# Filler matmuls in TensorE's idle stretches, bias rows by an eight-column matmul, more buffers for raw weights, and a new order

## The chip, the core and the metric

The kernel runs on one core of one Trainium2 chip. The metric is device time in microseconds (us). The kernel before was run three times: 3003.74, 3004.77 and 3006.28 us, so its median is 3004.77 us. The execution that the hardware profiler recorded took 3005.68 us; its instructions span 3004.0 us of that.

## What is computed

A stack of four graph layers works on 32 independent graphs ("batches") of 512 nodes with 128 features. Each graph has a 0/1 adjacency matrix `adj` of 512 x 512 with about 16 neighbours a node.

```python
h = relu(layernorm(x)); x = x + L0(h)   # max over neighbours j of relu(h@(W1-W2) at i + h@W2 at j + b)
h = relu(layernorm(x)); x = x + L1(h)   # 4 layers; each: src/dst aggregates by normalised adj, then
                                        #   tanh(concat(src_agg, self, dst_agg) @ wu + bu)
h = relu(layernorm(x)); x = x + L2(h)   # (adj / row sum) @ (h @ weight) + bias
h = relu(layernorm(x)); x = x + L3(h)   # 4 GRU steps: m = adj.T @ (h @ w3[l]); gates of m and h
# in L1: src = nodes @ ws + bs;  dst = nodes @ wd + bd;  self = nodes @ wn + bn
```

The weights are shared by all batches. In L1 the products `ws@wu`, `wn@wu` and `wd@wu` are formed once, and so are the bias rows `bs@wu` and `bd@wu`.

## The kernel before

`batch(b)` describes the whole work of one graph: `prepare` (load `x` and `adj`, first layer norm, a transposed adjacency `at`, counts `cc` copied across partitions into `ccd`, and the eight keys a row that name neighbours), `gathers` (28 gathers of rows `G` from a table in device memory by GpSimd, and 32 one-hot products `pa` by TensorE, both folded by maxima on VectorE into `gm` and `acc`), `layer1` (four layers with aggregates `pg` over `at` and `an`, and products `pu`), and `layer23` (layer 2, then four GRU steps with `pk`, `pg`, `phn` and `pxn`).

Nothing runs in the order in which it is written. `Flow` notes every operation with a cost and its dependencies. `step` then plays a small model of the five engines and issues, from those that could start first, the one with the earliest due time; `LEADS` shifts the due times of stages, `LAST` those of the last batches, and `PACE` sets the distance from batch to batch. Line 496 issues all of them, so nearly every row of the profile has line 496, and a row is told by its tiles. Each engine takes its instructions strictly in the order that comes out of this.

The weights enter the same flow as two more parts, `first` and `rest` (lines 1187 to 1188), with places `WEIGHTS` ahead of batch 0. In `rest`:

- the bias vectors are loaded into `brow` row by row, all on SyncE's DMA queue (line 663), transposed by one matmul `pb` and copied to `bcol`;
- for each of the four layers `wu`, then `ws`, `wn`, `wd` are loaded (lines 681 and 685), all three into the one buffer with the tag "f", transposed (`pwt`), copied (`wt`, tag "gate0"), multiplied (`pw`) and copied to `w1`;
- for each layer `pv` holds `bs@wu` and `bd@wu` as single rows of one partition. They are split into a rounded part and a remainder (`both`, lines 708 to 712), and eight small DMAs on SyncE's queue (lines 713 to 719) spread the four rows, twice each, over eight partitions of `b8`;
- then come the layer 2 weights, `w3`, and the eight GRU matrices `graw`, which share one buffer with the tag "gate1" (line 739).

The product `pu` of layer 1 reads `b8` with eight rows of scaling values `rows`. GRU step `l` of a batch is one long chain: transposes `ph`, rounding to `hi` and `lo`, eight passes `pg`, the copy `mT`, two `pk` and one `pxn` product, then `nn` and `h` on VectorE and ScalarE, and the next `ph`. The two first halves of `pk` and `phn` read only `h`.

PSUM has eight banks, shared by four users (`BANKS`, `Share`).

## Time and profile before

| item | value |
|---|---|
| median of 3 runs | 3004.77 us (3003.74 to 3006.28) |
| profiled execution | 3005.68 us, span 3004.0 us, mean granted TensorE clock 0.979 |
| TensorE matmul | 2821.0 us busy, 94% of the span |
| VectorE | 2403.8 us, 80% |
| GpSimd | 1798.9 us, 60% |
| ScalarE | 1214.9 us, 40% |
| chain that ended last | TensorE 77%, VectorE 12%, issue 4%, ScalarE 2%, DMA 1%, GpSimd 1% |

Times in the trace count from the start of the span. A busy time is the sum of an engine's instructions, and the granted clock is the share of full speed that the throttle gave TensorE. In the page's strip of 40 slices a slice is 75 us, and a digit is a tenth.

The batches can be followed by the group that writes `xo`, the last arithmetic of a batch: it ends its batches at 307.2 us (batch 0), 759.0 (batch 5), 2583.4 (batch 26), 2914.5 (batch 30) and 2993.1 (batch 31), each time the start of its fourth instruction. From batch 5 to batch 26 that is 1824.4 / 21 = 86.9 us a batch.

### The profile page before, as it was taken

The page shows a single profiled execution, that of the slowest core. Times are in us where ns is not written, and L with a number is a line of the kernel's source. Part 1 is how long each engine was busy: PE and PEld are TensorE (multiplying, and loading weights), DVE is VectorE, ACT ScalarE, POOL GpSimd, SP SyncE. Part 2 cuts the span into 40 slices and gives each one's busy share as a digit, 9 for nine tenths or more (in the row PEclk, how much of TensorE's full clock was granted, in tenths as well). Part 3 has the DMA queues.
Part 4 walks back from the last instruction along what each step waited for, and adds up shares of the span by engine and source line. Part 5 has one row for each costly group of instructions (what it writes and reads, how often), then busy time and mean ns, then how long its engine had stood idle before and what let it go on. Part 6 is the DMA issues. An engine that isn't in the chain of part 4 may idle for free.

```text
span 3004.0 us, 37228 instructions
## 1 busy us (share of the span) xinstructions
PE 2821.0 (94%) x11233; PEld 1741.0 (58%) x11233; DVE 2403.8 (80%) x5364; ACT 1214.9 (40%) x2516; POOL 1798.9 (60%) x2000
## 2 busy tenths in 40 slices
PE   4688989999999999999999999999999999999985
PEld 3455656666666666666666666666666666655542
DVE  5887879888888988888888888888988888886422
ACT  2333434444444434444444434444434444432322
POOL 3666666666666666666666666666666666655211
PEclk7899999999999999999999999999999999999997
DMA  5533343433344334333433433344333334333000
GB/s 142 122 80 67 77 84 74 82 69 67 71 85 85 81 73 84 60 64 86 85 83 73 85 61 71 76 84 85 75 80 79 66 64 85 67 57 58 11 4 5
DMA packets 192289, 218.42 MB, mean 73 GB/s; under 512 B 31401, under 2 KB 140625, under 8 KB 192081
## 3 DMA queue, kind: packets, MB, share of 16 engines
q0 software_dynamic: 47104, 92.34, 22.2%
q1 hardware_dynamic: 77392, 64.90, 7.2%
q10 hardware_dynamic: 67584, 58.73, 6.3%
q8 instruction: 91, 1.49, 0.2%
q14 instruction: 118, 0.96, 0.1%
HBM read 164.32 MB, written 17.96 MB: 61 GB/s over the span
## 4 chain that ended last, share of the span: by engine, by line
PE 77%; DVE 12%; issue 4%; ACT 2%; DMA 1%; POOL 1%; ACTq 0%; SPq 0%; DVEq 0%; POOLq 0%
PE pg L496 23%; PE pu L496 18%; PE pk L496 15%; PE pa L496 6%; PE phn L496 4%; PE pxn L496 4%; DVE acc L496 3%; PE pkey L496 2%; PE pf L496 2%; PE ph L496 1%; DVE qhl L496 1%; DVE nn L496 1%; DVE x L496 1%; PE pc L496 1%; PE pt L496 1%
## 5 line engine op out<-in xcount | busy, mean ns | idle before, releaser
L496 POOL DMA_INDIRECT G<-qtab,idx x768 | 824.6, 1074 | 602.6 <-DVE gm L496 487.9
L496 DVE TENSOR_TENSOR acc<-acc,pa 128x512 f32<-128x512 f32 x992 | 674.2, 680 | 146.7 <-PE pa L496 134.0
L496 PE MATMUL pa<-oh,qhl 128*128 128x512 f32 x1024 | 472.6, 515 | 12.5 <-DVE oh L496 6.7
L496 PE MATMUL pg<-an,hi 128*128 128x512 f32 x1024 | 461.3, 451 | 1.1 <-ACT hi L496 0.7
L496 PE MATMUL pu<-ag,w 128*128 128x512 f32 x896 | 449.9, 596 | 1.1 <-DVE ag L496 1.1
L496 PE MATMUL pg<-an,lo 128*128 128x512 f32 x1024 | 435.2, 426 | 0.7 <-POOL lo L496 0.7
L496 DVE TENSOR_SCALAR oh<-ccd 128x1024 fp32r<-128x1024 bf16 x512 | 401.2, 802 | 10.3 <-PE pa L496 10.3
L496 PE MATMUL pg<-at,hi 128*128 128x512 f32 x640 | 289.1, 452 | 13.9 <-ACT hi L496 9.2
L496 PE MATMUL pg<-at,lo 128*128 128x512 f32 x640 | 297.0, 465 | 3.4 <-POOL lo L496 2.8
L496 PEld LDWEIGHTS pa<-oh,qhl 128*128 128x128 f32 x1024 | 197.2, 194 | 147.0 <-issue 52.5
L496 PE MATMUL pk<-h,g_hh 128*128 128x512 f32 x512 | 262.7, 618 | 4.4 <-DVE acc L496 1.9
L496 DVE TENSOR_TENSOR gm<-gm,G 128x128 f32<-128x128 f32 x768 | 260.8, 340 | 3.9 <-DMA G<-qtab,idx 3.1
L496 ACT ACTIVATE xn<-x,shift,rstd 128x128 f32<-128x128 f32 x512 | 212.4, 484 | 110.1 <-POOL shift L496 109.4
L496 PEld LDWEIGHTS pg<-an,hi 128*128 128x128 f32 x1024 | 194.0, 189 | 95.5 <-issue 50.7
L496 PEld LDWEIGHTS pg<-an,lo 128*128 128x128 f32 x1024 | 193.9, 189 | 87.0 <-issue 40.9
L496 PE MATMUL pk<-mT,g_ih 128*128 128x512 f32 x512 | 240.8, 593 | 2.2 <-ACT mT L496 2.2
L496 ACT COPY mT<-pg 128x512 f32<-128x512 f32 x160 | 93.7, 585 | 354.6 <-PE pg L496 354.0
L496 PEld LDWEIGHTS pu<-ag,w 128*128 128x128 f32 x896 | 166.9, 190 | 114.5 <-issue 82.2
L496 ACT ACTIVATE gate<-pk,bsum 128x512 f32<-128x512 f32 x256 | 175.4, 686 | 139.2 <-PE pk L496 132.2
L496 POOL TENSOR_TENSOR rstd<-rstd,mhalf 128x4 f32<-128x4 f32 x128 | 145.9, 1140 | 139.4 <-DVE shift L496 138.6
L496 ACT CAST hi<-ph 128x512 fp32r<-128x512 f32 x96 | 56.2, 586 | 382.2 <-PE ph L496 382.2
L496 DVE TENSOR_TENSOR ag<-pg,rbc 128x512 f32<-128x512 f32 x256 | 174.5, 682 | 21.3 <-PE pg L496 18.2
(161 smaller groups left out, 5043.3 us busy)
## 6 DMA issues: line engine op xcount, KB each, us to landing
af<-in_adj_dram ACTq DMA_DIRECT2D x32, 1024.0 KB
ccd<-cc SPq DMA_DIRECT2D x512, 64.0 KB
an<-in_adj_dram POOLq DMA_DIRECT2D x128, 256.0 KB, 4.3
x<-in_x_dram ACTq DMA_DIRECT2D x64, 256.0 KB
rbc<-scal SPq DMA_DIRECT2D x32, 512.0 KB
G<-qtab,idx POOLq DMA_INDIRECT x768, 3.8
qtab<-qn SPq DMA_DIRECT2D x128, 64.0 KB
out_dram<-xo ACTq DMA_DIRECT2D x32, 256.0 KB
```

The costliest lines, as they stand in the source:

```text
L496: op.fn(*(real(v) for v in op.args), **{k: real(v) for k, v in op.kw.items()})
```

## The change

Five things change. `clock` is called before each TensorE instruction is placed: it issues `n` filler matmuls ("spin": constants times constants, 128x512, bf16, into an unused PSUM bank) when the model has TensorE idle for over 1 us, and it follows the throttle in the model, whose matmul costs now depend on it. The bias rows are made by matmuls with eight columns, `bm`, so that each row comes out on the partitions where it is wanted; the 32 small DMAs and the `both` tiles are gone. The raw weights get more buffers, and half of the weight loads go to ScalarE's DMA queue. `rest` is cut in two, with the later half, `last`, placed at -3.0. `PACE`, `LEADS` and `LAST` have new values, and so has the modelled cost of a DMA.

```diff
-PACE = 45.29
+PACE = 45.28
 LEADS = {
...
-    "gather0": 21.0, "gather1": 4.8, "gather2": 6.6, "gather3": -2.6,
-    "first": 14.3, "layer1": -15.8, "layer10": -31.7, "layer11": -34.7,
+    "gather0": 21.0, "gather1": 4.8, "gather2": 6.6, "gather3": -2.7,
+    "first": 14.9, "layer1": -15.8, "layer10": -31.7, "layer11": -34.7,
     "layer12": -17.6, "layer13": -49.5, "layer2": 17.3, "layer3": 7.8,
-    "layer30": 58.6, "layer31": 78.0, "layer32": 33.2, "layer33": 37.4,
-    "out": 22.6,
+    "layer30": 58.6, "layer31": 78.0, "layer32": 36.2, "layer33": 30.6,
+    "out": 18.1,
 }
-LAST = (0.0, 0.0, 0.06, -0.57, -0.08)
-WEIGHTS = (-4.52, -3.22)
+LAST = (0.0, 0.0, -0.31, -0.67, 0.62)
+WEIGHTS = (-4.52, -3.22, -3.0)
...
+    SPIN, IDLE = 0.23, 1.0
+    WINDOW = 3.413
...
-                return 0.4, 2.0 + outs[0].size() * width / 1.5e5
+                return 0.48 if engine == "sync" else 0.42, 2.0 + outs[0].size() * width / 1.2e5
...
+        if op.engine == "pe":
+            t = self.clock(op, t)
         cost = op.cost + (self.EVENT * max(0, len(need) - 1) if op.engine != "pe" else 0.0)
+        if op.engine == "pe":
+            cost /= self.rate
+            self.active += cost
...
+    def clock(self, op, t):
+        gap = t - self.free["pe"]
+        n = int(0.7 * (gap - 0.4) / self.SPIN)
+        if self.spin and gap > self.IDLE and n > 0:
+            ring = next(r for r in self.rings.values() if r.tag == "idle")
+            spare = [b for b in ring.slots if b is None or (not b.left and b.end < t)]
+            if spare:
+                view, work = self.spin(n)
+                buf = view.tile
+                buf.real = ring.give(buf)
+                for args in work:
+                    self.nc.tensor.matmul(*(real(v) for v in args), start=True, stop=True)
+                buf.end = t
+                self.active += n * self.SPIN
+        while t >= (self.window + 1) * self.WINDOW:
+            share = self.active / self.WINDOW
+            if share < 0.42:
+                self.rate = 0.5
+            elif share > 0.84:
+                self.rate = 1.0
+            self.window += 1
+            self.active = max(0.0, self.active - self.WINDOW)
+        return t
...
-            F.sync.dma_start(out=brow[at : at + m, :], in_=src)
+            (F.sync, F.act)[len(col) % 2].dma_start(out=brow[at : at + m, :], in_=src)
...
-        b8 = self.temp("hg", "b8")
+        self.b8 = self.own([8, NL1, P], F32R, "b8r")
+        bm = self.own([P, NL1, 2, 8], F32, "bm")
+        F.pool.memset(bm, 0.0)
+        for i in range(NL1):
+            for k, nm in enumerate(("bs", "bd")):
+                c = col[nm, i]
+                F.act.copy(bm[:, i, k, k::2], bcol[:, c : c + 1].to_broadcast([P, 4]))
...
-                w = self.temp("f", f"{nm}{i}")[:, 0:ch, :]
-                F.sync.dma_start(
+                w = self.temp(("f", "hg", "hT1")[k], f"{nm}{i}")[:, 0:ch, :]
+                (F.sync, F.act)[k % 2].dma_start(
...
-                wt = self.temp("gate0", f"wt_{i}_{k}")[:, 0:ch, :]
+                wt = self.temp(("gate0", "xn2")[k % 2], f"wt_{i}_{k}")[:, 0:ch, :]
...
-            for k, nm in enumerate(("bs", "bd")):
-                c = col[nm, i]
-                F.mm(pv[0:1, k, :], bcol[:, c : c + 1], wu[:, 2 * k, :], start=True, stop=True)
+            for k in range(2):
+                F.mm(
+                    pv[0:8, 0, :], bm[:, i, k, :], wu[:, 2 * k, :],
+                    start=(k == 0), stop=(k == 1), group=pv,
+                )
...
-            F.vec.tensor_copy(part, pv[0:1, 0:2, :].rearrange("p k d -> p (k d)"))
-            F.vec.tensor_sub(
-                both[0:1, 1, 0:256], pv[0:1, 0:2, :].rearrange("p k d -> p (k d)"),
-                both[0:1, 0, 0:256],
-            )
-            for h in range(2):
-                for g in range(2):
-                    for k in range(2):
-                        r = 4 * h + 2 * g + k
-                        F.sync.dma_start(
-                            out=b8[r : r + 1, i, :], in_=both[0:1, h, k * P : (k + 1) * P]
-                        )
-        self.b8 = self.own([8, NL1, P], F32R, "b8r")
-        F.vec.tensor_copy(self.b8, b8[0:8, :, :])
+            hi = F.tile(self.mid, [P, 4, P], F32R, "hi1", f"bhi_{i}", 1)[0:8, 0, :]
+            F.act.copy(hi, pv[0:8, 0, :])
+            full = self.temp("nn", f"bfull_{i}")[0:8, 0, :]
+            F.vec.tensor_scalar(full, pv[0:8, 0, :], self.sign[0:8, 1:2], None, ALU.mult)
+            F.vec.scalar_tensor_tensor(
+                self.b8[:, i, :], hi.bitcast(F32), self.sign[0:8, 0:1], full, ALU.mult, ALU.add
+            )
+    def last(self):
...
-                g = self.temp("gate1", f"graw_{nm}{l}")[:, 0:3, :]
-                F.sync.dma_start(
+                q = nm == "ih"
+                g = self.temp(("gate1", "xn1")[q], f"graw_{nm}{l}")[:, 0:3, :]
+                (F.sync, F.act)[q].dma_start(
...
+    def spin(n):
+        t = F.tile(ps, [P, NT, P], F32, "idle", "spin", 0)
+        return t, [(flat(t), W.identb, W.code.rearrange("p t d -> p (t d)"))] * n
+    F.spin = spin
...
-        [(WEIGHTS[0], W.first), (WEIGHTS[1], W.rest)]
+        list(zip(WEIGHTS, (W.first, W.rest, W.last)))
```

`sign` is a small constant written by four more GpSimd memsets: on partitions 0 to 3 it is (1, 0), on 4 to 7 it is (-1, 1), so that the first four rows of `b8` get the rounded value and the last four the remainder.

In the two compiled programs each engine's instructions can be laid side by side. The changed one has 257 filler matmuls: 138 before the repeating middle (84 of them before batch 0 has finished its one-hot products) and 119 from batch 29 on, the last 96 of these after the last transposes of batch 30. In the repeating middle, one batch takes the same instructions on every engine in both programs, and only a few neighbours are swapped.

## The prediction

> **What bounds the kernel now.** I read first the page's strip of TensorE and its clock, then a table of five windows, then shorter windows where TensorE is not full, then the chain of waits at the end.

> ```profile
> PE   4688989999999999999999999999999999999985
> PEclk7899999999999999999999999999999999999997
> ```

> Each digit is a tenth of a slice of 75 us, busy time above and granted clock below. The windows, with the busy time of TensorE, its weight loads, VectorE, ScalarE and GpSimd after the length, then granted clock, DMA share and GB/s:

> ```profile
> 0.00:150.00 150.00, 83.30 (x378) 55.64 (x379) 101.64 (x245) 42.92 (x111) 73.23 (x102) 0.81 0.56 132
> 150.00:300.00 150.00, 131.34 (x515) 79.33 (x514) 125.09 (x284) 57.16 (x122) 98.02 (x100) 0.95 0.37 73
> 300.00:2760.00 2460.00, 2409.82 (x9726) 1496.23 (x9725) 2085.59 (x4625) 1046.97 (x2165) 1577.81 (x1748) 1.00 0.38 75
> 2760.00:2900.00 140.00, 134.53 (x462) 77.60 (x461) 65.93 (x153) 46.35 (x83) 34.22 (x35) 1.00 0.05 14
> 2900.00:3004.00 104.00, 62.01 (x160) 32.18 (x158) 25.59 (x61) 21.46 (x36) 15.59 (x17) 0.77 0.02 6
> ```

> The middle is TensorE's: 2409.82 of 2460 us at full clock. Its order is nearly the same in both programs, so I leave 86.9 us a batch as it is; a swap could move it by some 0.1 us, 2 us in all. What can move lies at the ends: TensorE is idle for 66.7 + 18.7 us in the first 300 us and for 42.0 us in the last 104, and both are where its clock is low.

> **The tail.** Batch 31's last stage runs alone. Its chain is TensorE, ScalarE, VectorE in turn, and the clock has dropped.

> ```profile
> 2884.21 0.44 PE ph L496 x4
> 2884.65 1.72 PE pk L496 x4
> ...
> 2978.01 0.66 PE ph L496 x4
> 2978.67 2.78 PE pk L496 x4
> 2981.45 0.43 PE pg L496
> 2981.88 1.28 PE phn L496 x2
> 2983.16 1.63 PE pg L496 x7
> 2984.86 0.59 ACT mT L496
> 2985.50 1.99 PE pk L496 x4
> 2987.49 0.87 PE pxn L496 x2
> ```

> Columns: start, duration, what. The first two rows are the same work at full clock: `ph` x4 0.44 us, `pk` x4 1.72; from the same stretch, `phn` x2 0.86 and `pg` x8 1.84. Against these, the rows of batch 31 are too long by: `pg` and `po` of layer 2 1.8 + 1.6; GRU step 0 1.8; step 1 3.7; step 2 3.2; step 3 2.2 (0.2 + 1.1 + 0.2 + 0.4 + 0.3); last `ph` and the flag 0.5. Sum 14.8 us, nearly all on the chain.

> The change puts 96 fillers here in these gaps: 20 and 4 around the first `pg`, 13 before step 0, then 11 or 12 a step between `pxn` and `ph`, and twos beside `mT` and `hi`. A filler of 512 columns is not in the trace; the nearest row is a `pg` pass, 0.23 us at full clock (8 in 1.84) and 0.48 in the slow stretch (`pg` 3.37 us x7 at 2921.8). Twelve at 0.23 are 2.8 us; the gap from the end of `pxn` to `ph` is 3.3 us (2960.0 to 2963.3), so they fit, if the clock is up. They then fill about 85% of the gap, and it should stay up.

> [...] The rows show 9.6 us more, in steps 1 to 3 and the end, after gaps of 3.3 us. I go by the rows, less 2.8 us: the 20 fillers (4.6 us) leave some 2 us idle before `pg`, so the clock may still be down there (1.8), and the twos may each hold something up a little (1). **Tail: 12 us gained**, ends 5 and 14.8. The order of `pg`, `pk`, `pu` of batches 30 and 31 is otherwise the same, so the new `LAST`, "layer32" and "out" I cost at nothing. The 23 fillers at batches 29 to 31 before that (5 us at 0.23) stand against 5.5 us of idle time in 2760 to 2900; at worst half delays, 2 us.

> **The head.** Until about 200 us VectorE is the bound. Counting its instructions in the two programs with the mean spacing of each kind in the trace (`acc` 0.60 us, `oh` 0.60, `gm` 0.20, `junk` 2.2), the work before batch 0's first `oh` is 14 us before and 16 after, before batch 1's first `oh` 68 and 66, before batch 2's 102 and 100, before batch 0's `x2` 153 and 155. So the head moves only by VectorE's idle time. In the trace these four come at 35.8, 109.1, 151.9 and 207.3 us: idle 22, 41, 49 and 54 us so far. The 32.5 us after the first `oh` lie here:

> ```profile
> 40.00:50.00 10.00, 3.42 (x10) 2.05 (x9) 5.98 (x12) 0.53 (x2) 6.63 (x8) 0.81 0.54 98
> 50.00:60.00 10.00, 5.69 (x16) 2.98 (x16) 5.52 (x14) 0.27 (x1) 4.18 (x5) 0.53 0.79 210
> ```

> The timelines of SyncE's queue and of TensorE (start, duration, what, and in brackets the idle time before and what ended it) name two causes:

> ```profile
> 56.43 4.97 SPq L496 DMA_DIRECT2D b<-both  x8
> ```

> ```profile
> 105.36 0.88 PE L496 MATMUL pg_hh<-ident,graw_hh 128*128 128x128 f32 x3 [4.43 <-DMA graw_hh<-in_L_gnn_w_hh_dram]
> ...
> 123.85 0.87 PE L496 MATMUL pg_hh<-ident,graw_hh 128*128 128x128 f32 x3 [5.08 <-DMA graw_hh<-in_L_gnn_w_hh_dram]
> ```

> - **Bias rows.** Removed: 32 DMAs, 0.6 us of SyncE's queue each (4.97 / 8), 8 for each layer, of which the first 8 stand before `ccd` of blocks 2 and 3; 8 `both` instructions of 0.41. Added: 8 copies into `bm` and 4 `bhi` on ScalarE, at about 0.27 (the copy of `w`) 3.2 us, beside an idle ScalarE (0.27 us busy in 50 to 60); 8 VectorE instructions on 8 partitions at about 0.2 (the `code` copies), less than removed; the matmuls replace as many; four more memsets, 0.1 each.
> - **Weights.** `wd` at 52.8 us keeps TensorE waiting 5.9 us and with it `pa` and VectorE, since its load could start only when the shared buffer was free; `graw_hh` does the same twice, 4.4 and 5.1 us. With separate buffers, and most of SyncE's loads issued before `qtab` and `ccd`, these go. Of 8.5 us of idle VectorE in 40 to 60 I count 7 as gained; of 14.4 us in 80 to 130 (windows of 10 us: 2.5, 2.5, 3.2, 2.7, 3.5) half, 7. What is late next there is the chain keys, `ccd`, `oh` of batch 1: the new order has 11, 17 and 9 fillers around it, so TensorE waits there still.
> - **The start is later.** ScalarE's queue now issues `wn` and eight `brow` loads before `af` (1 MB) and `x`, and VectorE does four `wt` before `junk`. Before: `af` issued at 0.8, `junk` at 8.6, but batch norm only at 19.6, behind `pb`, which waited until 18.9 for `brow`; the first `pat` at 23.2. After: `brow` on two queues. [...] 9 of 18 loads at 0.29 us (the rows 14.36 to 17.28) are 2.6 us, `pb` at 16.3. The trace adds that `brow` could start only at 8.3, when `af` had landed, and that goes: I take `pb` at 14, behind 25 fillers that wait for `code` (written at 12.3 before, behind `junk`; now ahead of it, near 6; 25 at 0.23 to 0.48 are 6 to 12 us). Then four rounds of `pwt`, `wt`, `pw` of about 1.2 us: `junk` 19, `pat` 25.5. From `pat` to `oh` it was 12.6 us; the new VectorE order adds four `wt` (1.2) and batch 1's `junk` (2.2): first `oh` at 41.5. With 16 us of work done then, idle 25.5 against 22: 4 us lost.

> **Head: 7 + 7 - 4 = 10 us gained**; ends -6 (fillers at the slow clock, nothing regained at batch 1) and +18. After that TensorE's order is the same up to a few swaps, and I carry the 10 us to the end.

> **Sum.** Span 3004.0 - 12 - 10 = 2982. The profiled execution took 1.7 us more than its span and 0.9 more than the median, so the median is 2983.

> **Rivals.**
> 1. *Only the tail gains* (20 in 100). Batch 0's start is later by more than the waits give back: with `pat` at 30 and half of the 14 regained, the head is -1 to 0: 2993. For it: the load of `af` moves behind ten others. Against it: `junk` was not what held batch 0; `pb` was.
> 2. *The whole of both* (18 in 100): VectorE idles no more than 4 us after the first `oh`, and low-clock windows in 187 to 276 go: 3004 - 14 - 20 = 2970.
> 3. *Fillers outlast the gaps, slower* (5 in 100). If the clock stays low, 12 fillers at 0.48 are 5.8 us in a gap of 3.3: each of four steps loses 2.5, so 10, nothing is gained in the tail, and the start loses 6: 3021. The point from which it decides is 3.3 / 12 = 0.275 us a filler. Against it: the clock was back at full within each step of batch 31 even without fillers (`pk` 1.99, `pxn` 0.87).
> 4. *The fillers don't raise the clock* but cost nothing, and the head cancels (7 in 100): 3002 to 3008.

> The forecast has 50 in 100. **Range 2966 to 2997**: from somewhat beyond rival 2 to rival 1 and its error. A measurement of this kernel tells 0.2%, 6 us, from no change: faster 0.88, same 0.07, slower 0.05.

> **What would show it.** Clock near 1.00 after 2900, GRU steps of about 12 us where they took 13.7 to 15.2, `pk` x4 at 1.72; the middle at 86.9 us a batch; no waits for `graw_hh` over 2 us; first `oh` after 40 us but batch 0's `x2` near 197; `xo` of batch 5 near 749. I am wrong in the tail if the clock stays under 0.9 there, in the head if `x2` of batch 0 comes after 205, and in the whole if the pace in the middle moves.

## The result, and the profile after

The changed kernel took 2975.73 us (median of 4 runs, 2971.70 to 2976.73), the kernel before 3005.49 beside it: a ratio of 0.9899, interval [0.9882, 0.9916]. Two repetitions on other chips gave 0.9900 [0.9885, 0.9916] and 0.9912 [0.9898, 0.9926]. The profiled execution took 2976.68 us with a span of 2975.0, which is 29.0 less than the 3004.0 of before.

The page's strips of TensorE and its clock:

```profile
PE   7789999999999999999999999999999999999997
PEclk9989999999999999999999999999999999999999
```

Each digit is a slice of 74 us. The 4, 6 and 8 at the start have become 7, 7 and 8, and the 5 at the end a 7. Part of that is filler and no work, so the windows matter more. Columns: busy time of TensorE, its weight loads, VectorE, ScalarE and GpSimd, granted clock, DMA share, GB/s.

```profile
0.00:150.00 150.00, 117.89 (x585) 68.97 (x585) 117.38 (x286) 51.85 (x136) 80.16 (x115) 0.93 0.64 139
150.00:300.00 150.00, 139.07 (x506) 82.13 (x506) 118.41 (x275) 56.32 (x122) 101.40 (x106) 0.92 0.44 86
300.00:2760.00 2460.00, 2414.36 (x9750) 1499.80 (x9748) 2081.91 (x4633) 1046.59 (x2166) 1582.01 (x1727) 1.00 0.37 74
2760.00:2870.00 110.00, 106.98 (x366) 60.39 (x365) 46.26 (x106) 36.66 (x67) 38.65 (x41) 1.00 0.14 18
2870.00:2975.00 105.00, 83.40 (x290) 41.48 (x288) 29.35 (x66) 24.63 (x41) 17.57 (x19) 0.95 0.02 6
```

VectorE now does 117.38 us of work in the first 150, where it did 101.64. The clock of the first window rose from 0.81 to 0.93, that of the last stretch from 0.77 to 0.95; in the second window, 150 to 300, it did not rise (0.95 before, 0.92 now). The middle is as full as it was.

Times of the same instruction in the two profiles show where the 29 us came from (`oh` is a one-hot of the neighbours, made on VectorE for TensorE; `x2` is the `x` after layer 1, the row `x<-px,x`; `xo` is the last arithmetic of a batch):

| instruction | before | after | gain so far |
|---|---|---|---|
| first `oh`, batch 0 | 35.8 | 42.4 | -6.6 |
| `x2`, batch 0 | 207.3 | 196.6 | 10.7 |
| `x2`, batch 1 | 310.6 | 290.2 | 20.4 |
| `xo`, batch 5 | 759.0 | 737.4 | 21.6 |
| `xo`, batch 26 | 2583.4 | 2562.3 | 21.1 |
| `xo`, batch 30 | 2914.5 | 2895.3 | 19.2 |
| `xo`, batch 31 | 2993.1 | 2964.1 | 29.0 |

So 21.6 us come in the first batches, nothing in the middle (1824.9 us from batch 5 to 26, 1824.4 before), 1.9 are lost in batches 27 to 30, and batch 31, which ends alone, gains 9.8. The chain of waits of that end (start, duration, what):

```profile
2902.55 3.25 PE pg L504 x7
...
2939.25 1.72 PE pk L504 x4
2940.97 0.24 PE pg L504
2941.20 0.86 PE phn L504 x2
2942.06 1.61 PE pg L504 x7
2943.75 0.59 ACT mT L504
2944.39 1.98 PE pk L504 x4
2946.37 0.87 PE pxn L504 x2
```

The first `pk` x4 takes 1.72 us, as at full clock; it was 2.78 in the step quoted in the prediction. One dip of the clock is left before the end of the work, at layer 2's `pg` x7 (3.25 us), with 2.4 us without a filler (2898.6 to 2901.0) ahead of it.

### The profile page after: what moved, and what is told of

Read it like the earlier page. It is cut to its first block, busy times and chain, and to the rows that moved or that the text cites. A ratio compares the mean times of both kernels' runs of the same rounds, so it can differ in the third digit from the quotient of the medians.

```text
span 2975.0 us, 37664 instructions
## 1 busy us (share of the span) xinstructions
PE 2861.7 (96%) x11490; PEld 1752.8 (59%) x11490; DVE 2393.3 (80%) x5363; ACT 1216.1 (41%) x2528; POOL 1819.8 (61%) x2005
## 3 DMA queue, kind: packets, MB, share of 16 engines
q0 software_dynamic: 47104, 92.34, 22.5%
## 4 chain that ended last, share of the span: by engine, by line
PE 78%; DVE 12%; issue 4%; DMA 2%; ACT 2%; POOL 2%; DVEq 0%; SPq 0%; ACTq 0%; POOLq 0%
PE pg L504 23%; PE pu L504 18%; PE pk L504 15%; PE pa L504 6%; PE pxn L504 4%; PE phn L504 4%; DVE acc L504 3%; PE pkey L504 2%; PE ph L504 2%; PE pf L504 1%; DVE nn L504 1%; DVE qhl L504 1%; PE pt L504 1%; DVE oh L504 1%; DVE x L504 1%
## 5 line engine op out<-in xcount | busy, mean ns | idle before, releaser
L504 POOL DMA_INDIRECT G<-qtab,idx x768 | 840.8, 1095 | 574.5 <-DVE gm L504 461.5
L504 PE MATMUL pa<-oh,qhl 128*128 128x512 f32 x1024 | 472.1, 512 | 10.8 <-DVE acc L504 6.6
L504 DVE TENSOR_SCALAR oh<-ccd 128x1024 fp32r<-128x1024 bf16 x512 | 392.2, 783 | 13.6 <-PE pa L504 12.6
```

What stands on the lines that cost most here:

```text
L504: op.fn(*(real(v) for v in op.args), **{k: real(v) for k, v in op.kw.items()})
```

## What the experiments had to tell apart

The prediction's theory (A) had the first batches, the head, gain because weight loads and bias rows no longer hold up VectorE, and had fillers matter only in the tail, where the last batch runs alone. But twice as much was gained there as it said. The rival (B) is that fillers help the first batches too, by keeping TensorE's clock up. Two smaller questions: what the new order of batches 27 to 31 is worth, and whether more fillers bring more.

The twelve runs were made in three sets of four, each set on one chip with its own runs of the kernel before (3004.06, 3004.61 and 3004.09). Executions of one kernel differ by up to 12.5 us in a set, so medians are given, and a set's kernels are compared with one another first.

## Fillers taken out, everywhere and by halves

In `clock` the matmuls alone are left out; the planner still counts them, so that all engines get the same instructions in the same order.

```diff
# e1_no_fillers: the loop over work is removed
# e2_fill_tail, e2b_fill_tail:
-                for args in work:
+                for args in work if t > 2000.0 else ():
# e3_fill_head: t < 2000.0
```

> The changed kernel without any of the 257 fillers (the planner's books are kept, so every other instruction has the same order). Theory A, the gain in the first 500 us comes from the weight loads and bias rows, and fillers matter only in the tail: the tail's 10 us are given back, about 2986, batch 0's x2 still near 197 and batch 5's xo within 2 us of 737, GRU steps of batch 31 back to 13.7 to 15.2. Rival B, the fillers also give the head by keeping TensorE's clock up: another 11 (the part gained after batch 0's x2) to 21 us go, 2997 to 3006, and batch 5's xo lies at 748 to 758.

> The changed kernel with only the 119 fillers after batch 29, none in the first 500 us. Theory A: as the changed kernel, 2974 to 2978, batch 5's xo near 737. Rival B: 11 to 21 us slower, 2987 to 2997. A third possibility, that the 84 fillers ahead of batch 0's one-hot hold up the start: some us faster, 2970 to 2974, with batch 0's first oh ahead of 41.

> The changed kernel with only the 138 fillers ahead of the middle, none in the tail. Theory A: the tail's 10 us are given back, 2986, last four h about 15, 14.7, 13.7 us apart as before. [...] Rival B expects 2986 too, here the two don't part.

Measured, first set: without fillers 2999.93 (2993.91 to 3006.39, ratio 0.9988 [0.998, 0.9997]), tail only 2990.06 (0.9959 [0.9946, 0.9972]), head only 2992.31 (0.9965 [0.9952, 0.9978]). The first two lie where rival B put them (2997 to 3006 and 2987 to 2997); head only is 6 us above the 2986 of both theories. From no fillers, adding the tail's brings 9.9 us, adding the head's 7.6, and without any the change keeps only 4 us. The profile of the kernel without fillers tells what loads, bias rows and order give by themselves, and when:

| instruction | before | no fillers | changed |
|---|---|---|---|
| `x2`, batch 0 | 207.3 | 204.4 | 196.6 |
| `x2`, batch 1 | 310.6 | 300.3 | 290.2 |
| `xo`, batch 5 | 759.0 | 748.2 | 737.4 |

Without fillers 3 us are gained by batch 0's `x2`, but 10.8 by batch 5, which is the 10 us that A's sum for the head gave; 4.9 of them are lost again after it, most of it in batches 27 to 30 (333.2 us for 331.1) and in the lone part (81.2 for 78.6). The other half of the head's gain came with the fillers. Single profiles scatter: without the head's fillers the three on record have `xo` of batch 5 at 745.6 to 749.4, with them five have it at 737.4 to 746.3.

The tail first. With no fillers there the lone part of batch 31 (`xo` of batch 30 to that of batch 31) took 81.2 and 78.7 us in the two profiles; in the profiles with fillers it is 67.5 to 71.3. The chain of waits of the head-only kernel shows a step as it was before:

```profile
2953.66 1.08 PE ph L504 x4
2954.74 3.41 PE pk L504 x4
2958.16 0.43 PE pg L504
2958.59 1.18 PE phn L504 x2
2959.76 1.63 PE pg L504 x7
2961.47 0.59 ACT mT L504
2962.11 1.98 PE pk L504 x4
2964.09 0.87 PE pxn L504 x2
```

Here `pk` x4 takes 3.41 us for 1.72, `ph` x4 1.08 for 0.66. The last four `h` (the new state that ends a GRU step) are 14.4, 14.7 and 13.7 us apart (2938.47, 2952.82, 2967.52, 2981.25); with fillers 13.0, 12.0 and 12.0. The tail's low end of 5 us in the prediction was its author's estimate, and it is too small here. The clock went down at 2938.6, 2952.3 and 2969.3 us (its mean was 0.73 in 2925 to 2940, 0.84 in 2940 to 2955 and 0.81 in 2955 to 2975), and in the 3.4 us before these moments TensorE was busy for 0.69, 1.35 and 0.94 us.

The head was compared once more, with the changed kernel on the same chip.

> The changed kernel, reference of this set: 2976 as twice before if the chip makes no difference; about 2982 if the first set's chip was slow and this is it again.

> The changed kernel with only the 119 fillers after batch 29 once more, now beside the changed kernel on one chip. Theory B, as the sets so far compare: fillers in the first 500 us are worth 14 us (2990 against 2976). If that comparison was one of two chips and the gains simply add: 8 us. Theory A: below 3 us.

Measured: 2979.88 (2975.45 to 2983.87) and 2991.18 (2984.22 to 2991.82, ratio 0.9951 [0.9937, 0.9966]): 11.3 us for the 138 fillers of the head, between the 7.6 and the 14 that the sets had suggested. Theory A's "below 3" is out. The gains of head and tail don't simply add: 9.9 + 7.6 would bring 2999.9 to 2982, and the changed kernel took 2975.91 and 2979.88 in the other two sets. Why is open. Windows of the changed kernel in that set:

```profile
0.00:50.00 50.00, 37.06 (x189) 21.48 (x191) 23.05 (x72) 19.22 (x59) 10.04 (x35) 0.86 0.59 167
50.00:100.00 50.00, 40.93 (x214) 24.87 (x217) 47.75 (x113) 12.78 (x30) 33.65 (x42) 0.93 0.79 157
```

And of the kernel with fillers in the tail only:

```profile
0.00:50.00 50.00, 22.70 (x124) 16.12 (x125) 21.06 (x68) 18.77 (x57) 8.79 (x34) 0.92 0.57 163
50.00:100.00 50.00, 35.20 (x172) 24.43 (x170) 45.51 (x106) 12.96 (x32) 30.87 (x39) 0.80 0.69 139
```

Read the third engine column: VectorE, the bound of this stretch, has done 70.80 us of work after 100 us with the fillers (23.05 + 47.75) and 66.57 without. The instructions are the same; TensorE, which feeds it, runs at 0.93 in place of 0.80 between 50 and 100. (The clocks of the first window, 0.86 and 0.92, compare badly: their records begin at 9 us in the one trace and at 32 in the other.) By batch 0's `x2` the difference is 4.1 us (197.8 against 201.9), by batch 5's `xo` 3.7 (742.0 against 745.6). The two executions profiled are the slowest of the one kernel's five and the fastest of the other's (2983.87 and 2984.22 us), so they show how the head gains, but not the whole of the 11.3.

## The weights' code put back

```diff
# e5_one_buffer
-                w = self.temp(("f", "hg", "hT1")[k], f"{nm}{i}")[:, 0:ch, :]
-                (F.sync, F.act)[k % 2].dma_start(
+                w = self.temp("f", f"{nm}{i}")[:, 0:ch, :]
+                F.sync.dma_start(
# and so for brow, wt and graw
# e6_bias_dma: b8 by both and 32 DMAs again, b8's buffer in "nn", loads as changed
# e11_old_weights: rest and last with all of this as before
```

> The changed kernel once more, as the reference of this set. The first set makes head fillers worth about 8 us (all fillers out 2999.9, tail only 2990.1, head only 2992.3, so 9.8 and 7.6) and the sum of both 17.5, so 2982 if the two add up on this chip; 2975 to 2977, as it ran at first, if they help each other or the chip of the first set was slower.

> The changed kernel with the raw weights of layer 1 and 3 in one buffer each and all their loads on SyncE's queue, as before; bias rows by matmul and fillers stay (283 fillers). Theory A, as the prediction had it: TensorE waits for wd and graw_hh again, 9 to 11 us slower than the changed kernel and batch 5's xo later by as much. Rival D, the waits are mostly hidden, since VectorE has other work and fillers keep the clock: within 3 us of it.

> The changed kernel with the bias rows of layer 1 formed and moved by 32 DMAs as before, raw buffers and two queues stay (271 fillers). Theory A: the 32 DMAs take 20 us of SyncE's queue in the stretch 40 to 130 us, ahead of ccd and so of the one-hots: 3 to 7 us slower than the changed kernel. Rival D: SyncE's queue has room, within 2 us of it.

> The changed kernel with the weights' code wholly as before (one queue, one buffer, bias rows by 32 DMAs), the fillers and the planner's clock stay (281 fillers). Theory A: the loads and bias rows are worth 10 us by themselves, 10 slower than the changed kernel, near 2992. Rival B, the gain in the first 500 us is the clock's: within 4 us of the changed kernel. If the two need each other (fillers fit only once the waits are short): over 14 us slower.

Measured: the changed kernel 2975.91 (2971.89 to 2981.93); one buffer 2988.20 (2984.25 to 2989.71, ratio 0.9943 [0.993, 0.9957]), 12.3 slower; bias by DMA 2994.12 (2990.66 to 2997.83, 0.9965 [0.9953, 0.9978]), 18.2 slower; both as before 2987.09 (2985.17 to 2988.75, 0.9942 [0.9928, 0.9956]), 11.2 slower. In size, one buffer and both together are near what A said. Bias by DMA came out at more than twice the most that either theory allowed, and the parts don't add. All three are planned anew, so an edit's cost includes the new places that the plan gives to everything else. What the split of `rest`, the modelled clock and DMA cost and the new `LEADS` of the head are worth by themselves was not tested.

The window in which the one-buffer kernel loses most of VectorE's work is this:

```profile
75.00:100.00 25.00, 19.46 (x126) 13.67 (x127) 12.91 (x33) 11.63 (x30) 12.04 (x18) 0.86 0.60 117
```

and what TensorE waited for in and near it (idle before and releaser in brackets):

```profile
46.34 0.48 PE L504 MATMUL pwt<-ident,wd 128*128 128x128 f32 x1 [4.04 <-DMA wd<-in_L_gnn_wd_dram]
...
92.02 1.09 PE L504 MATMUL pw3t<-ident,w 128*128 128x128 f32 x4 [1.78 <-DMA w<-in_L_gnn_weight_dram]
...
122.31 0.55 PE L504 MATMUL pg_hh<-ident,graw_hh 128*128 128x128 f32 x3 [1.69 <-DMA graw_hh<-in_L_gnn_w_hh_dram]
```

VectorE works 12.91 us of 25 here, where the changed kernel has 23.66 in the same window. The wait of `wd` is back; those of `graw_hh` are not (1.69 us, where before had 4.4 and 5.1). The keys of batch 1 are late, but by their place in the new order: its `junk`, the first step to them, starts at 77.7 us for 39.9 in the changed kernel's first profile, without a wait before it. The clock has little to do with it: adding up the low stretches in the clock records of the first 500 us gives 41 us for this kernel and 58 for the changed one's profile of that set. This window is not the whole account of the 12.3. At batch 3's `x2` the one-buffer kernel is ahead again (470.6 us, where two profiles of the changed kernel have 473.1 and 478.4); only at batch 4's is it behind for good (572.8, against 561.6 and 566.9), long after its last weights are copied at 142.9.

For the bias rows SyncE's queue shows one cause (start, duration, what):

```profile
24.41 5.03 SPq L504 DMA_DIRECT2D b<-both  x8
...
35.64 5.14 SPq L504 DMA_DIRECT2D b<-both  x8
40.88 2.03 SPq L504 DMA_DIRECT2D qtab<-qn  x4
43.00 7.45 SPq L504 DMA_DIRECT2D ccd<-cc  x11
```

Sixteen small DMAs, 10.2 us of the queue, now stand ahead of batch 0's first `qtab` and `ccd`. In the changed kernel `qtab` is issued at 34.36 and `ccd` at 37.21. Batch 0's first `oh` comes at 47.2 us for 42.4 to 43.3. That explains some 4 us. Then this kernel too is ahead at batch 3's `x2` (463.6) and behind at batch 4's (574.6). So how much of either cost is waiting for weights and small DMAs, and how much the other order that the planner chose, is not shown.

## The old order of the last batches

```diff
-LAST = (0.0, 0.0, -0.31, -0.67, 0.62)
+LAST = (0.0, 0.0, 0.06, -0.57, -0.08)
# and layer32, layer33, out as before
```

> The changed kernel with the old values of LAST, layer32, layer33 and out (36.2, 30.6, 18.1 back to 33.2, 37.4, 22.6), which move only batches 27 to 31. Theory A, the new order of these batches costs the 1.9 us that batches 27 to 31 lost against before: 2974, faster than the changed kernel by 1 to 3. Rival C, the new order pays for itself with the fillers and the faster tail: 2977 to 2982, and the lone part at the end grows as batch 31's first row comes earlier.

Measured: 2983.50 (2978.42 to 2988.02, ratio 0.9938 [0.9927, 0.995]). This set held no run of the changed kernel, and that varies from chip to chip by some 4 us (2975.73, 2975.91 and 2979.88), so the times don't decide it, though 2983.50 lies above both expectations. In the profiles batches 27 to 30 take 331.6 us with the old values, as before (331.1), and 333.0, 334.2 and 334.2 in three of the changed kernel; the lone part takes 70.4 against 68.9, 68.8 and 71.3. So the new order costs 1.4 to 2.6 us in batches 27 to 30, and whether it gives them back in the lone part stays open.

## More fillers

```diff
# e9_more_fill (e13_more_head: only where t < 2000.0)
-                for args in work:
+                more = int(0.95 * (gap - 0.2) / self.SPIN)
+                for args in work[:1] * more:
```

> The changed kernel with more fillers in the same places, 95% of the predicted gap less 0.2 us in place of 70% of it less 0.4 (399 for 257), every other instruction in the same order. In the tail about 17 for 12: 3.9 us in a gap of 3.3, so each of three to four steps loses 0.6 and rival 3 of the prediction sets in, less 1.8 us for the low window before layer 2's pg that goes: 0 to 1 us slower there. In the first 500 us 1 to 4 us faster, if low clock is what is left; 2 to 6 slower, if fillers already stand in front of the work there. Sum: 2972 to 2976 by the first, 2978 to 2983 by the second.

> The changed kernel with more fillers in the first 500 us alone (331 in all), the tail's as they are. If low clock is what is left there: 1 to 4 us faster than the changed kernel, the best of all, with fewer low windows than its 48 us; if fillers already stand in front of the work: 2 to 6 slower.

Measured: 2982.84 (2978.17 to 2984.80, ratio 0.9924 [0.9909, 0.9939]) and 2982.82 (2977.89 to 2985.00, 0.9928 [0.9915, 0.9942]), beside 2979.88 for the changed kernel: not faster, and the intervals overlap. "1 to 4 faster" is out; "2 to 6 slower" fits the medians, not clear of noise. In the profile with more fillers everywhere, low stretches in the first 500 us add up to 17 us, and `xo` of batch 5 comes at 737.1. The changed kernel has 58 us of them and 742.0 in its profile of the set, but 48 us and 737.4 in its first: with a third of the low clock left, the head was no earlier than there, though the profile with more fillers is the fastest of its five. So the head's gain does not go on growing as the low clock goes; whether further fillers then stand in front of work was not traced. In the tail both of the expected effects are seen:

```profile
2904.61 1.78 PE pg L504 x7
...
2936.77 2.97 PE spin L529 x13
2939.74 0.44 PE ph L504 x4
2940.18 1.72 PE pk L504 x4
```

The last dip is gone, `pg` x7 at 1.78 for 3.25, and now the chain of waits runs through fillers: `ph` follows 13 of them directly. A step takes 12.3 us (`ph` at 2939.74 and 2952.04), where the changed kernel has 12.1 (2938.59 and 2950.65), so an overrun costs about 0.2 us a step, not 0.6. No version beat the changed kernel.

## Why the prediction was right, and what it mis-sized

**Result.** 2983 was forecast, 2976 measured, within the range and a little nearer to rival 2's 2970. Rivals 3 and 4 are out, and so is rival 1: the head did gain. The total is close in part by luck, since the tail gave 4 us less than said and the head 11.6 more.

**Tail: 12 forecast, 7.9 in the profiles.** The lone part, which the sum of over-long rows was about, gave 9.8; the fillers alone, put in, 9.9. Steps of 12.0 us and `pk` at 1.72 came as said, and so did the dip before layer 2's `pg`. The step that failed is "the new `LAST`, 'layer32' and 'out' I cost at nothing": batches 27 to 30 take 1.9 us longer, and the profiles with the old values bear that out. The other 2.2 is the sum itself, which let every row go back to full clock: the second `pk` of a step still takes 1.98 us for 1.72 and `ph` 0.64 for 0.44, over four steps (0.26 + 0.20) x 4 = 1.8. The prediction took `pk` at 1.99 for full clock in rival 3, and for 0.3 too long in the sum; with the clock at 1.00 (2905.6 to 2966.8) it stayed at 1.98.

**Head, the term that was mis-sized: 10 forecast, 21.6 measured.** Its single steps were near: first `oh` 42.4 us (41.5 forecast), `junk` 21.8 (19), `pat` 28.0 (25.5), so that idle VectorE before `oh` grew by 3.1, from 22.5 to 25.6 (4 forecast); idle VectorE in 40 to 60 fell from 8.5 to 0.1 us (7 counted as gained, 8.4 seen), in 80 to 130 from 14.4 to 3.4 (7 counted, 11.0 seen). `x2` of batch 0 was at 196.6 for "near 197", but that is luck: in the three profiles without the head's fillers it is at 201.2 to 204.4, so 4.5 to 7.7 of the 10.7 us gained by then are the fillers', which the sum had not counted. Another sentence failed with it: "After that TensorE's order is the same up to a few swaps, and I carry the 10 us to the end". Other batches are already under way at that point, and they hold more to gain: 10.7 at batch 0's `x2` is 20.4 at batch 1's. Between the two TensorE idles 11.9 us before and 6.1 in the changed kernel, and most of this second step is there without fillers (3.0 and 10.4 us gained). `xo` of batch 5 came at 737.4 where "near 749" was said; without fillers it comes at 748.2. `x2` of batch 0 is a poor witness altogether: the one-buffer kernel has it at 194.7, sooner than any, and ends 12 us later.

**Why it was mis-sized.** Fillers stood in the head's sum only as a cost, "behind 25 fillers", since VectorE is the bound there. But VectorE did less work where TensorE fed it at a lower clock: between 50 and 100 us 45.51 us at a mean clock of 0.80, without the head's fillers, and 47.75 at 0.93 with them. Taken away, the head's fillers cost 7.6 and 11.3 us, the loads and bias rows 11.2; together 19 to 23, about what the head gained, though parts of a plan need not add. Rival 2 had named this ("low-clock windows in 187 to 276 go") and its 20 us for the head were about right, though not the place: 168 to 185 and 253 to 260 us stayed low, and VectorE idles 14.3 us between the first `oh` and batch 0's `x2`, where it said no more than 4.

**Middle.** 86.9 us a batch, as forecast. The longest wait for `graw_hh` is 2.12 us, where under 2 was said.

## What to carry to other kernels

Where the bound engine is fed by TensorE, price filler matmuls there as well as where TensorE works alone: in this kernel the head's fillers were worth 7.6 and 11.3 us, the tail's 9.9. Fillers for 70% of the predicted gap paid here, and 95% gained nothing more (2982.84 us beside 2979.88). Read a gain in a software pipeline where it has become steady, not at the first batch's milestone, and compare regenerated schedules only with what is kept equal, since an edit that makes the planner choose anew brings its own order with it.

## What the hardware showed beside this

The time differs between executions of one program. The changed kernel took 2971.89 us at a mean clock of 0.991 and 2981.93 at 0.988 on one chip, and its `xo` of batch 5 lay at 737.4, 742.7 and 742.0 in three profiles. Whether the clock causes this scatter is not shown: on another chip it took 2975.45 us at 0.990 and 2980.08 at 0.992.
